# Chunks turned by VectorE's 32x32 transposes from rows loaded by quarters, and a landing wait at every fourth indirect transfer

## The chip, the cores and the metric

One core of a Trainium2 chip. The metric is the device time in microseconds, the median of several runs of the whole program. In the text PE is TensorE (the matrix engine), DVE is VectorE, ACT is ScalarE, POOL is GpSimd, and SP is SyncE, which here only issues transfers. "L374" is line 374 of the kernel.

## What is computed

The input `x` is 4 images of 32 channels, 128 x 128, float32. Layer 0 regroups each image into 128 channels (32 x 2 x 2) of 4096 pixels (64 x 64) and attends over the pixels: a 4096 x 4096 matrix of cosines, its softmax, and a weighted sum. Layer 1 takes the result as 4096 tokens of 128 per image: it is a linear attention without softmax, then a mixture of 8 experts with 2 chosen per token.

```python
def _L0_conv_ref(x, gamma):
    ...
    xs = x.reshape(B, C, h, R, w, R).transpose(0, 1, 3, 5, 2, 4).reshape(B, C * R * R, h, w)
    q = xs.reshape(B, C * R * R, hw)
    energy = jnp.einsum('bci,bcj->bij', q, q)
    d = jnp.sqrt(jnp.diagonal(energy, axis1=1, axis2=2))
    energy = energy / (d[:, :, None] * d[:, None, :])
    attn = jax.nn.softmax(energy, axis=-1)
    out = jnp.einsum('bcj,bij->bci', q, attn).reshape(B, C * R * R, h, w)
    out = gamma * out + xs
...
def _L1_attn_ref(x, Wk, Wq, Wv):
    ...
    KtV = jnp.einsum('bhnk,bhne->bhke', K, V)
    out = jnp.einsum('bhnk,bhke->bne', Q, KtV)
...
def _L1_ffn_ref(x, router_w, router_b, expert_w, expert_b):
    router_probs = jax.nn.softmax(x @ router_w + router_b, axis=-1)
    top_p, top_i = jax.lax.top_k(router_probs, K)
    top_p = top_p / jnp.sum(top_p, axis=-1, keepdims=True)
    expert_out = jnp.einsum('bnd,edc->bnec', x, expert_w) + expert_b
    ...
# layer 0, then for tokens t of its result:
    t = t + _L1_attn_ref(_ln_t(t), ...)
    t = t + _L1_ffn_ref(_ln_t(t), ...)
```

## The kernel before

**Layer 0.** For each of the 4 images the 4096 pixels are cut into 8 chunks of 512 (`NCH = 8`, `CH = 512`), and a chunk into 4 blocks of 128 (`NJ = 4`). Two forms of each chunk are kept: `qn`, channels by pixels with each pixel's vector scaled to length 1, and `qT`, pixels by channels, unscaled. `attend` (L416) walks over pairs of chunks (i, jc) with jc up to i: L557 makes the energies `pe` of one block against a chunk, L560 their exponentials `pr` on ACT with row sums, and L439 multiplies them with `qT` into `po` two steps later. The matrix is symmetric, so the other triangle is not computed. Instead L368 transposes `pr` in 32x32 blocks on DVE, L482 writes the result to a buffer in DRAM, and L494 reads it back with the 32-row groups exchanged, in six transfers on SP's queue. L374 (L395 for a diagonal tile) multiplies the returned tile, and L384 (L404) adds the product to the accumulator `o`. That use is scheduled `LAG = 57` units of a running count of matmul work after the read-back is issued.

**Preparing the chunks.** `prep(b, kc, st)` (L281) makes two chunks at a time, so it runs four times per image. It loads rows of the image in four transfers (`load_tokens`, L278), transposes them on PE in two groups of four 128x128 (L312), evicts each group on DVE into `qT` (L301), takes squares and row sums on DVE (L323, L324), raises the sums to the power -1/2 on POOL (`rn`, L163), scales `qT` into `qs` on DVE (L337), transposes `qs` back on PE in two groups of four (L345) and copies each to `qn` on ACT (L343). For the first chunk 22 filler transposes (`keep_running`) run on PE meanwhile.

**The order of work.** The order on PE, DVE, ACT and SP is the order in which the program emits it. The loop at L1348 steps through `attend`, whose every step yields twice, and at both it advances the streams that are due. A timed stream has a begin and an end, in per cent of the image's attention work, and a count: it comes due at even spacing, `count` times between the two, and is advanced twice each time. So a stream that yields n times is over after about n/2 counts. The preparation of the next image's chunks 0 and 1 runs late in an image, that of its chunks 2 and 3 early in the next.

**Layer 1** (L603) of an image runs as another stream beside the attention of the next image. It divides layer 0's accumulator (L710) and adds it to the tokens `T` (L732), normalises, attends, and chooses the experts. `sorted_experts` (L921) sorts the tokens of each half of an image by expert: 32 indirect transfers on POOL (L996) scatter rows of 128 tokens into `xs` in DRAM; SP loads the sorted tiles (L1022) once all have landed; PE transposes them (L1065) and multiplies them with the chosen expert (L1058); the products go to `ys`, and 32 more indirect transfers (L1123) gather them into `yb`; DVE combines (L1092). Each of these indirect transfers already waits for the exponential that was emitted last (`exps`), so that there are not more of them than attention steps. The last image's layer 1 takes another way, without sorting. `input_rows` (L594) loads the tokens `T` of an image.

Of the kernel before, what the change touches and what calls it, by code (L numbers as in the profile page):

```python
# [22 lines left out]
def kernel(  # L23
# [43 lines left out]
    nc = tc.nc  # L67
# [60 lines left out]
    def wait_for(inst, others, why):  # L128
        for other in others:
# [3 lines left out]
            )  # L133

# [146 lines left out]
    def prep(b, kc, st):  # L281

        if b == 0:
            if kc == 0:
                st["all"] = big1.tile([P, 4, 8, HW2, 2], F32, tag="T", name="xx_0")
            xx = st["all"][:, kc]
        else:
            xx = xin.tile([P, 8, HW2, 2], F32, tag="xx", name=f"xx_{b}_{kc}")
        first = b == 0 and kc == 0
        load_tokens(  # L290
            xx.rearrange("p k w r -> p k (w r)"), b, 8 * kc, 8, (nc.sync, nc.scalar if first else nc.sync)
        )
# [3 lines left out]
        yield  # L296
        yield
        yield from idle(2 if b else 1)

        def load_half(g, pt):  # L300
            nc.vector.tensor_copy(  # L301
                qT[:, :, 2 * g : 2 * g + 2, :].rearrange("p s j (r c) -> p (j r) s c", c=64),
                pt.rearrange("p (m s c) -> p m s c", s=2, c=64),
            )

        for g in range(2):
            yield
            pt, done = hold(f"ptq_{b}_{kc}_{g}", partial(load_half, g))
            for jj in range(2):
                for r2 in range(2):  # L310
                    k = 4 * g + 2 * jj
                    nc.tensor.transpose(  # L312
                        pt[:, ts(2 * jj + r2, P)], xx[:, k : k + 2, :, r2].rearrange("p k w -> p (k w)"), ident
                    )
            yield
            done()
        yield
# [3 lines left out]
        for s in range(2):  # L321
            sq = work.tile([P, NJ, P], F32, tag="qs", name=f"sq_{b}_{kc}_{s}", bufs=2)
            nc.vector.tensor_tensor(sq, qT[:, s], qT[:, s], ALU.mult)  # L323
            nc.vector.tensor_reduce(ss[:, ts(s, NJ)], sq, AX.X, ALU.add)  # L324
            if first:
                pow_neg_half(rn[:, ts(s, NJ), 0], ss[:, ts(s, NJ)])
            elif s == 1:
                pow_neg_half(rn[:, :, 0], ss)
            yield
            yield  # L330
        yield from idle(1)
        if first:
            keep_running(22, ps_g, "pg")
        scaled = []
# [1080 lines left out]
```

## Time and profile before

| | us |
|---|---|
| median of 3 runs | 1706.01 (1704.19 to 1707.77) |
| the profiled execution, its time | 1708.28 |
| the profiled execution, its span | 1706.5 |
| PE / DVE / ACT / POOL busy, 14 to 350 us (attention of image 0) | 333.8 / 141.9 / 168.5 / 9.0 |
| 350 to 757 us (image 1, layer 1 of image 0) | 399.0 / 232.9 / 226.7 / 142.5 |
| 757 to 1163 us (image 2) | 397.0 / 233.7 / 222.0 / 146.0 |
| 1163 to 1570 us (image 3) | 397.0 / 222.6 / 221.7 / 145.7 |
| 1570 to 1706 us (the last layer 1) | 118.3 / 98.8 / 84.4 / 65.1 |

The granted clock of TensorE is 0.994 over the span. The stretches of images are set by hand; an engine's busy time is the union of its instructions in the stretch. How the lines of the profile are read: a group line names the source line, engine, operation, what is written and read, the shapes and how many; then the busy time of the group, the mean of one in ns, and the idle time of the engine just before them with what ended it. A line of the timeline begins with start and duration.

### The profile page before, as it was taken

The numbers are of one execution on the slowest core, as the hardware profiler recorded it, in microseconds if no ns is written. First come the engines' busy times: TensorE is split into PE (matmuls) and PEld (weight loads), VectorE is DVE, ScalarE is ACT, GpSimd is POOL, SyncE is SP. The second block draws the span as 40 slices with busy tenths as digits, with TensorE's granted clock in tenths as the row PEclk, the third lists the DMA queues.
The fourth block names the chain that finished last, engine by engine and source line by source line (L and its number), as shares of the span: only waits on it lengthen the run. The fifth ranks groups of instructions, "written<-read, shape, count | busy, mean of one in ns | idle before, by whom it ended". The sixth has DMA issues, their size and how long they took to land.

```text
span 1706.5 us, 21941 instructions
## 1 busy us (share of the span) xinstructions
PE 1652.0 (97%) x5458; PEld 874.7 (51%) x5458; DVE 935.0 (55%) x2443; ACT 925.2 (54%) x2893; POOL 512.2 (30%) x553
## 2 busy tenths in 40 slices
PE   8999999999999999999999999999999999999898
PEld 5444544455554555445554455545555455544543
DVE  4433334467485345478477334557748533454686
ACT  3555445566565555446565455545657455544476
POOL 1000000011026425460015632443102642435157
PEclk9999999999999999999999999999999999999999
DMA  4554756754458778875457677886445877885001
GB/s 134 168 179 154 207 178 210 248 182 162 163 167 265 221 244 239 251 234 161 146 172 239 221 249 235 244 249 186 162 153 168 261 223 225 246 244 145 7 9 42
DMA packets 227341, 323.94 MB, mean 190 GB/s; under 512 B 31760, under 2 KB 155792, under 8 KB 213136
## 3 DMA queue, kind: packets, MB, share of 16 engines
q1 hardware_dynamic: 206704, 283.57, 52.5%
q0 software_dynamic: 12288, 25.19, 5.2%
q10 hardware_dynamic: 8224, 13.77, 2.8%
q8 instruction: 46, 0.75, 0.2%
q14 instruction: 79, 0.65, 0.1%
HBM read 152.28 MB, written 173.15 MB: 191 GB/s over the span
## 4 chain that ended last, share of the span: by engine, by line
PE 75%; DVE 9%; DMA 4%; issue 4%; ACT 4%; SPq 3%; POOL 1%; another core or an unknown queue 1%; ACTq 0%; DVEq 0%; POOLq 0%
PE pe L557 21%; PE po L439 21%; PE pg L374 17%; PE pys L1058 3%; PE py L1207 2%; PE pg L395 2%; SPq L494 2%; PE pys L1065 1%; DVE F L368 1%; PE pat L803 1%; DMA blocks<-F 1%; DMA F<-blocks 1%; ACT xn L645 1%; PE pgram L677 1%; DVE df L710 1%
## 5 line engine op out<-in xcount | busy, mean ns | idle before, releaser
L560 ACT ACTIVATE pr<-pe 128x512 f32<-128x512 f32 (+1 forms) x576 | 322.4, 560 | 548.9 <-PE pe L557 419.8
L439 PE MATMUL po<-pr,qT 128*128 128x512 f32 (+3 forms) x1152 | 552.2, 561 | 6.5 <-ACT o L444 6.0
L557 PE MATMUL pe<-qn,qn 128*128 128x512 f32 x896 | 462.3, 598 | 5.1 <-ACT pr L560 4.8
L374 PE MATMUL pg<-F,qT 128*128 128x512 f32 x864 | 441.9, 593 | 0.8 <-DMA F<-blocks 0.8
L368 DVE STREAM_TRANSPOSE F<-pr 128x512 f32<-128x512 f32 x440 | 306.1, 702 | 173.8 <-ACT pr L560 149.4
L439 PEld LDWEIGHTS po<-pr,qT 128*128 128x128 f32 x1152 | 216.1, 191 | 253.8 <-issue 223.0
L379 ACT ACTIVATE junk<-F 128x512 bf16<-128x512 f32 x432 | 267.9, 620 | 0.9 <-DMA F<-blocks 0.9
L374 PEld LDWEIGHTS pg<-F,qT 128*128 128x128 f32 x864 | 164.5, 191 | 193.8 <-issue 179.7
L1123 POOL DMA_INDIRECT yb<-ys,place x192 | 185.7, 967 | 252.8 <-ACT pr L560 72.6
L996 POOL DMA_INDIRECT xs<-xn,place x192 | 186.5, 971 | 162.3 <-ACT pr L560 83.7
L557 PEld LDWEIGHTS pe<-qn,qn 128*128 128x128 f32 x896 | 153.8, 191 | 114.5 <-issue 98.9
L384 DVE TENSOR_TENSOR o<-o,pg 128x512 f32<-128x512 f32 x110 | 75.4, 685 | 190.5 <-PE pg L374 153.3
L163 POOL TENSOR_TENSOR rn<-ss,neg_half 128x8 f32<-128x8 f32 (+1 forms) x17 | 26.9, 1586 | 332.2 <-DVE ss L324 332.1
L560 ACT ACTIVATION_READ_ACCUMULATOR pr<-pe 128x1 f32 x576 | 112.2, 195 | 0.0
L1032 ACT ACTIVATE xn<-pys 128x256 f32<-128x256 f32 x120 | 45.3, 378 | 112.6 <-PE pys L1065 80.7
L163 POOL TENSOR_TENSOR rsf<-dm_f,neg_half 128x8 f32<-128x8 f32 (+1 forms) x15 | 26.2, 1744 | 233.7 <-DVE sv_f L637 233.7
L1058 PEld LDWEIGHTS pys<-ew_sb,xn 128*128 128x128 f32 x468 | 69.4, 191 | 47.5 <-issue 43.1
L557 PE MATMUL pe<-qn 128*128 128x512 f32 (+3 forms) x256 | 90.5, 436 | 0.7 <-ACT qn L343 0.7
L379 ACT ACTIVATION_READ_ACCUMULATOR junk<-F 128x1 f32 x432 | 82.8, 192 | 0.0
L163 POOL TENSOR_TENSOR rsa<-dm_a,neg_half 128x8 f32<-128x8 f32 x16 | 26.4, 1649 | 185.3 <-DVE sv_a L637 184.9
L1041 DVE COPY xn<-pys 128x256 f32<-128x256 f32 x60 | 25.4, 424 | 91.1 <-ACT xn L1032 65.9
L1058 PE MATMUL pys<-ew_sb,xn 128*128 x468 | 71.8, 275 | 0.2
(216 smaller groups left out, 1623.5 us busy)
## 6 DMA issues: line engine op xcount, KB each, us to landing
blocks<-F SPq DMA_DIRECT2D x108, 1024.0 KB
F<-blocks SPq DMA_DIRECT2D x216, 192.0 KB
F<-blocks SPq DMA_DIRECT2D x216, 128.0 KB
xn<-xs SPq DMA_DIRECT2D x114, 128.0 KB
F<-blocks SPq DMA_DIRECT2D x216, 64.0 KB
below<-F SPq DMA_DIRECT2D x31, 384.0 KB
out_dram<-acc SPq DMA_DIRECT2D x128, 64.0 KB
xx<-in_x_dram SPq DMA_DIRECT2D x62, 128.0 KB
```

The costliest lines, as they stand in the source:

```text
L163: pinned(nc.gpsimd.tensor_tensor(dst, src, neg_half.to_broadcast(list(src.shape)), ALU.pow))
L368: f()
L374: nc.tensor.matmul(pg.rearrange("p (a f) -> p a f", a=4), st["qT"][i][:, ib, :], G[:, :, ib], start=(ib == 0), stop=(ib == NJ - 1),)
L379: nc.scalar.activation(junk, G[:, :, ib], AF.Copy, accum_out=st["sums"][:, NJ * i + ib, jc : jc + 1])
L384: nc.vector.tensor_tensor(o, o, pg.rearrange("p (a j c) -> p a j c", a=4, c=S), ALU.add)
L439: nc.tensor.matmul(row["po"][:, lo:hi], qT[blk // NJ][:, blk % NJ, :], w, start=start, stop=(row["left"] == 0))
L557: nc.tensor.matmul(pe[:, c0:], qn[jc][:, ts(j, P)], qn[i][:, c0:], start=True, stop=True)
L560: nc.scalar.activation(pr[:, c0:], pe[:, c0:], AF.Exp, accum_out=sums[:, t, i : i + 1]).ins
L996: inst = nc.gpsimd.indirect_dma_start(xs[h], offset(place[:, i, k : k + 1]), xn[:, k, :], None)
L1032: nc.scalar.activation(bufs[4 + g % 2][:, :n], p[:, : n * P].rearrange("p (j t) -> p j t", t=P), AF.Copy)
L1058: nc.tensor.matmul(p[:, 2 * P + j * D : 2 * P + j * D + D], bufs[4 + g % 2][:, j, :], weights[:, bass.ds(begins[2 * (g % 2) + j], D)], sta ...
L1123: inst = nc.gpsimd.indirect_dma_start(yb[k // 4][:, i, k % 4, :], None, ys, offset(place[:, i, k : k + 1]))
```

## The change

Chunks are made in another way, and the indirect transfers get another wait.

1. `load_quarters` loads the rows of two chunks in four transfers so that a quarter of the image rows stands on 32 partitions, 2 KB contiguous per row group, into one buffer `xa` (the pool's single buffer, shared with `xx`). `turn_quarters` makes `qT` of it with four 32x32-block DVE transposes of 128x256. The PE transposes at L312 and their evictions are gone. The pixels within a chunk now stand in another order, which `in_order` and `in_turn` and new access patterns in the division follow; the addition of L384 becomes contiguous, and the copies of `po` and the additions of `back` become permuted.
2. For all but the very first chunks, `qn` is no longer transposed from a scaled `qT`. The rows are loaded a second time, as before (`load_tokens` into `xx`; for image 0 straight into `T`), the factors `rn` are widened on DVE, transposed on PE in one group of four, and four DVE products of 64x512 read them from PSUM. The two ACT copies are gone.
3. The first chunks have their own `prep_first`, which still transposes `qn` on PE, with 40 filler transposes.
4. `T` of image 0 is loaded during the preparation; `input_rows` runs for images 1 to 3 only.
5. The preparation streams have new begins, ends and counts.
6. `landed_by_fours`: over both kinds of indirect transfer and all images, each fourth transfer waits until the one before it has landed.

```diff
+    moves = []
+
+    def landed_by_fours(inst):
+        if moves and len(moves) % 4 == 0:
+            wait_for(inst.ins, moves[-1:], "every fourth waits for all before it")
+        moves.append(inst.ins)
...
+    def load_quarters(b, kc, queues=(nc.sync, nc.sync)):
+
+        xa = xin.tile([P, 2, 2, 2, HW2, 2], F32, tag="xx", name=f"xa_{b}_{kc}")
+        halves = x[b].rearrange("c (s g) w -> c s (g w)", s=2)
+        for a in (0, 2, 1, 3):
+            first_row = 16 * kc + 4 * a
+            queues[a // 2].dma_start(
+                xa[ts(a, S)].rearrange("p s k r w e -> p s (k r w e)"),
+                halves[:, :, first_row * W : (first_row + 4) * W],
             )
-        for g in range(2):
-            yield
-            pt, done = hold(f"ptq_{b}_{kc}_{g}", partial(load_half, g))
-            for jj in range(2):
-                for r2 in range(2):
-                    k = 4 * g + 2 * jj
-                    nc.tensor.transpose(
-                        pt[:, ts(2 * jj + r2, P)], xx[:, k : k + 2, :, r2].rearrange("p k w -> p (k w)"), ident
-                    )
...
+    def turn_quarters(s, xa, qT):
+        for k in range(2):
+            nc.vector.transpose(
+                qT[:, s, 2 * k : 2 * k + 2, :].rearrange("p h (e r c) -> p r (h e) c", e=2, r=2),
+                xa[:, s, k].rearrange("p r (h t) e -> p (r h) e t", h=2),
+            )
+
+    def prep_first(st):
...
+        for s in range(2):
+            turn_quarters(s, xa, qT)
+            squares(b, kc, s, qT, ss)
+            pow_neg_half(rn[:, ts(s, NJ), 0], ss[:, ts(s, NJ)])
+        keep_running(40, ps_g, "pg")
...
+    def prep(b, kc, st):
+        ahead = 2 if b == 0 and kc == 1 else 5
+        xa = load_quarters(b, kc)
+        if b == 0:
+            load_tokens(st["T"][:, ts(kc, 8), :], b, 8 * kc, 8)
+            xx = rows_of_image(b, kc, st)
+        for _ in range(ahead):
+            yield
+        qT = chunks_of(b, kc, st)
+        for s in range(2):
+            turn_quarters(s, xa, qT)
+            yield
+        if b > 0:
+            xx = xin.tile([P, 8, HW2, 2], F32, tag="xx", name=f"xx_{b}_{kc}")
+            load_tokens(xx.rearrange("p k w r -> p k (w r)"), b, 8 * kc, 8)
...
+            for r2 in range(2):
+                nc.vector.tensor_tensor(
+                    qn[ts(r2, 64)].rearrange("p (j a t) -> p a j t", a=4, t=S),
+                    xx[own].rearrange("p (a k) (h t) r -> p r a (k h) t", a=4, h=2)[:, r2],
+                    view(spread[own]),
+                    ALU.mult,
+                )
...
+        for s in range(2):
+            squares(b, kc, s, qT, ss)
+            if s == 1:
+                pow_neg_half(rn[:, :, 0], ss)
+            yield
+        for _ in range(ahead - 2):
+            yield
+        wide = work.tile([P, NJ, 2, 64], F32, tag="qs", name=f"wide_{b}_{kc}", bufs=2)
+        for s in range(2):
+            nc.vector.tensor_copy(wide[:, :, s], rn[:, ts(s, NJ)].to_broadcast([P, NJ, 64]))
         yield
...
+        bank, done = hold(f"pnorm_{b}_{kc}", scale_all)
+        for j in range(NJ):
+            nc.tensor.transpose(bank[:, ts(j, P)], wide[:, j].rearrange("p s c -> p (s c)"), ident)
+        yield
+        done()
         yield
...
-                o = st["o"][jc].rearrange("p (j a c) -> p a j c", a=4, c=S)
-                nc.vector.tensor_tensor(o, o, pg.rearrange("p (a j c) -> p a j c", a=4, c=S), ALU.add)
+                nc.vector.tensor_tensor(st["o"][jc], st["o"][jc], pg, ALU.add)
...
-                    nc.scalar.activation(o, row["po"], AF.Copy)
+                    nc.scalar.activation(in_order(o), in_turn(row["po"]), AF.Copy)
...
                 wait_for(inst.ins, exps, "not more of these at a time than steps have")
+                landed_by_fours(inst)
                 scatters.append(inst.ins)
...
                 wait_for(pinned(inst).ins, exps, "not more of these at a time than steps have")
+                landed_by_fours(inst)
...
-            for kc, begin, end in ((1, 0, 5), (2, 6, 20), (3, 25, 45)):
-                timed.append((prep(0, kc, states[0]), begin, end, 12))
+            for kc, begin, end in ((2, 6, 22), (3, 25, 48)):
+                timed.append((prep(0, kc, states[0]), begin, end, 16))
...
-            timed.append((prep(b + 1, 0, nxt), 65, 82, 13))
-            timed.append((prep(b + 1, 1, nxt), 87, 99, 13))
-        begin, end, count = (52, 94, 17) if b == 0 else (36, 47, 9)
-        timed.append((input_rows(b, states[b]), begin, end, count))
+            timed.append((prep(b + 1, 0, nxt), 52, 78, 16))
+            timed.append((prep(b + 1, 1, nxt), 80, 99, 16))
+        if b > 0:
+            timed.append((input_rows(b, states[b]), 36, 47, 9))
...
-            timed.append((prep(b + 1, 2, nxt), 2, 20, 13))
-            timed.append((prep(b + 1, 3, nxt), 30, 50, 13))
+            timed.append((prep(b + 1, 2, nxt), 1, 22, 16))
+            timed.append((prep(b + 1, 3, nxt), 28, 52, 16))
```

## The prediction

> **What bounds the kernel.** I read the page's busy times and chain first, then the order of time on TensorE (PE) around its longest gaps, then the costs by form, then GpSimd's (POOL) indirect transfers.
>
> ```profile
> PE 1652.0 (97%) x5458; PEld 874.7 (51%) x5458; DVE 935.0 (55%) x2443; ACT 925.2 (54%) x2893; POOL 512.2 (30%) x553
> ...
> PE 75%; DVE 9%; DMA 4%; issue 4%; ACT 4%; SPq 3%; POOL 1%; another core or an unknown queue 1%; ACTq 0%; DVEq 0%; POOLq 0%
> ```
>
> PE is the bound: 97% busy, three quarters of the chain that ended last. Only PE time that goes, or a PE wait that comes or goes, moves the end. Busy time is not PE's price, though, because matmuls overlap; the distance between starts is. In order of time (start, duration, instruction, count, idle time before it):
>
> ```profile
> 721.34 1.02 PE L374 MATMUL pg<-F,qT 128*128 128x512 f32 x2
> ...
> 724.57 0.72 PE L312 MATMUL ptq<-ident,xx 128*128 128x128 f32 x4 [2.22 <-DMA xx<-in_x_dram]
> 725.13 1.02 PE L557 MATMUL pe<-qn,qn 128*128 128x512 f32 x2
> ...
> 727.71 0.63 PE L312 MATMUL ptq<-ident,xx 128*128 128x128 f32 x4
> 728.17 1.02 PE L557 MATMUL pe<-qn,qn 128*128 128x512 f32 x2
> ...
> 743.21 1.02 PE L374 MATMUL pg<-F,qT 128*128 128x512 f32 x2
> 747.30 0.66 PE L345 MATMUL ptn<-ident,qs 128*128 128x128 f32 x4 [3.07 <-issue]
> 747.79 1.46 PE L557 MATMUL pe<-qn,qn 128*128 128x512 f32 x2
> 749.04 1.91 PE L439 MATMUL po<-pr,qT 128*128 128x512 f32 x2
> 750.75 1.48 PE L374 MATMUL pg<-F,qT 128*128 128x512 f32 x2
> ```
>
> Two things are seen here. A group of four transposes moves the next matmul by 0.46 us (727.71 to 728.17), not by its 0.63; over all groups the median is 0.467 for L312 and 0.437 for L345. A pair of 128x512 records takes 0.86. And two of the worst PE gaps stand ahead of just these transposes: one waits for the input load, the other for VectorE (DVE). After the second, PE runs slowly for a while (749.04 to 750.75 is 1.71 in place of 0.86).
>
> **TensorE work that goes.** Each of the 15 later chunks loses four groups (two L312, two L345: 2 x 0.467 + 2 x 0.437 = 1.81 us) and gains one (0.437, as L345): 1.37 x 15 = **-20.6 us**. As busy time, the same 12 transposes of some 0.16 us would be 28 us; I take the pitch. The Trainium skill, VectorE: DVE Perf Modes, The three transpose paths, gives TensorE 390 ns for a 128x128 bf16 transpose; by that the 180 that go would be 70 us. No row here shows such a price in a stream, and it enters nothing.
>
> **TensorE waits that go.** Four stalls belong to the old chunk: at 721.34 (3.79 us to the second next start, where 0.86 + 0.467 are needed: 2.5 lost), 743.21 (7.54 to 750.75, 3.02 needed: 4.5), and their like one batch on, 1125.80 to 1133.58 (4.7) and 1150.12 to 1156.68 (4.4): 16.1 us. The first kind can't return in that form, since no PE instruction reads the input any more. The second is DVE's backlog from the division of layer 1 (L710, 2.78 us, then T L732, 1.22) falling on the last chunk's scaling. The new code moves that chunk: batch 1 runs from about 350 to 757 us (its four pow instructions of `rn`, at 407.6, 527.3, 657.5 and 738.7, stand at 14, 43, 76 and 95% of it), and the stream is advanced twice a count, so 15 yields end after 8 of 16 counts: at 90% (716 us) instead of 99%, ahead of the division at 739. Bounds: 0 (the new group waits for DVE's widening just as long) to -16.1. I take **-12**, nearer to the full amount, because the clash in time is gone, and leave 4 for new ones.
>
> **Start.** First matmul of attention now at 13.68 us. New: data at about 5.5, as now (again four loads of 128 KB, two on each queue), transposes 0.42 x 2 for the first half, squares 0.65 + 0.69, again for the second half, then one scaling (0.69): 5.5 + 4.4 + 0.7 = 10.6; four transposes 0.5, copy 0.6: 11.8. So -1.9 there. The 40 filler transposes end near 2 + 40 x 0.194 = 9.8 (the identity is ready at 1.8, and 22 took 4.27 now), just in time. But the second chunk's load shares its one buffer with the first, so SyncE's queue holds it to about 8.5 and it lands near 12; its norms then come at about 19.8, when PE asks at about 19.4. I take **-1.5**, bounds -2.5 and +3.
>
> **VectorE and ScalarE.** Costs by form (count, busy us, mean ns, idle before):
>
> ```profile
> L368 DVE STREAM_TRANSPOSE F<-pr 128x512 f32<-128x512 f32 x440 | 306.1, 702 | 173.8 <-ACT pr L560 149.4 <-issue 12.5 <-DMA F<-below 7.5
> ...
> L514 DVE STREAM_TRANSPOSE F<-pr 128x128 f32<-128x128 f32 x186 | 44.2, 283 | 22.8 <-ACT pr L560 20.1 <-issue 2.1 <-DMA F<-blocks 0.2
> L710 DVE TENSOR_TENSOR df<-o,pbd 64x512 f32<-64x512 f32 x64 | 44.0, 687 | 7.5 <-PE pbd L723 3.7 <-PE pe L557 2.6
> ...
> L337 DVE TENSOR_TENSOR qs<-qT,rn 128x512 f32<-128x512 f32 x32 | 20.6, 682 | 1.5 <-POOL rn L163 1.5
> ...
> L701 DVE TENSOR_SCALAR rdx<-rd,gam 128x256 f32<-128x256 f32 x32 | 10.5, 370 | 0.6
> ```
>
> Gone per chunk: two evictions (L301, 0.68) and two scalings (0.68), 2.72 us. Added: four 128x256 transposes (between L514's 0.28 and L368's 0.70; linear in columns gives 0.42, as taken: 1.68), two widenings (as L701, 0.37: 0.74), four 64x512 products out of PSUM (as L710, 0.687: 2.75). That is 5.17, so +2.45 x 15 = 37 us of DVE, from 935 to 972 (57%). At the transposes' upper bound it is 54. It costs nothing on the path: DVE idles 43% and works behind PE by the slack of six `pr` buffers. If that cover went, up to 37 us would show. ScalarE (ACT) loses two copies of 0.60 per chunk, 18 us, also hidden. The contiguous `o` additions (110 x 0.685) and the permuted copies (0.590) I leave at their old price: between 0 and -3 us for DVE, by the contiguous L323 row (0.656), off the path.
>
> **Loads.** Four more 128 KB loads per chunk of batches 1 to 3 (6 MB, SyncE issue of 0.45 us each), against 32 input loads of batch 0 that go (2 MB): under 2% of 324 MB. A load can hold SyncE's queue for the DVE transposes ahead of it (up to 3 us) and behind it wait L482 and L494, the round trip of the exponentials. Taken as 0: see the slack next.
>
> **The landing waits.** POOL and SyncE now:
>
> ```profile
> 550.21 0.96 POOL L996 DMA_INDIRECT xs<-xn,place  x1 [0.30 <-issue]
> ...
> 566.55 0.96 POOL L996 DMA_INDIRECT xs<-xn,place  x1 [5.26 <-ACT pr L560]
> ...
> 553.24 1.72 SPq L1022 DMA_DIRECT2D xn<-xs  x2
> 557.67 2.91 SPq L494 DMA_DIRECT2D F<-blocks  x6
> ```
>
> From the trace's packets (32 per transfer, in order) an indirect transfer lands 1.86 to 5.9 us after its start, mean 3.2. Back to back, starts are 1.27 apart. So four take 3 x 1.27 + 3.2 + 0.25 (the semaphore wait, an assumption from the 0.30 gaps) = 7.3 us, where the pace set by the exponentials is 6.2 (30 transfers from 502.13 to 548.95). Carrying every recorded start forward under the new rule, the last one of a half slips 9 to 12 us in the three first-half scatters, under 1 in the second-half ones, 3 to 8 in the six gathers: 68 us in all. What is queued behind: on POOL the pow instructions; on SyncE the load L1022 at 553.24, which waits for the scatter's landing and would move to about 563, and behind it L494 at 557.67. Cover: those blocks are first read by PE at 577.4 (shares are taken in order), 19.7 us after issue, while six transfers take some 6; the sorted rows are transposed at 569.2, 15.6 after their load ends; DVE's combine (L1092) comes 5 to 13 us after the landing of its row in most cases, 2.5 at the least. So nearly all is hidden: I take **+3**, bounds 0 and +68.
>
> The Trainium skill, DMA: Bandwidth & Descriptors, Anatomy of one DMA, gives a software-issued transfer 2.0 us + bytes/436e3, 2.15 us here. By it four would take 6.2, no lag at all; the trace's 3.2 differs and decides, and the page's figure enters no term.
>
> **Sum.** -20.6 - 12 - 1.5 + 3 = -31.1 us on the profiled execution (span 1706.5, time 1708.28): 1677.2. Its time is 2.27 above the median of the runs (1706.01), so the forecast for the median is **1675**.
>
> **Rivals.** (A) *The landing waits reach PE.* If a loaded queue lands the waited transfer about 1 us later than now, the gather halves (seven waits each) eat their 5 to 8 us of slack, DVE stands still in L1092, the transposes behind it come late, and PE follows. For: POOL already starts back to back for long stretches. Against: the slack above. With nothing hidden, 1675 - 3 + 68 = **1740**; it turns slower than before from about 34 us uncovered. 0.22. (B) *VectorE takes over* where slices show it at 8 tenths: its 37 us are paid, 1675 + 37 = **1712**, and 1706 if part of it. Against: the L384 and L368 rows wait for others 190 and 174 us. 0.07. (C) *The stalls only move*: PE waits as long for the widening as it did for L337; 1675 + 12 = **1687**. 0.15. That the new code doesn't do what it says I exclude: each removed transpose stands in the diff.
>
> **How the numbers follow.** Forecast 0.56, with its own range 1665 to 1684: at the low end all 16.1 us of stalls go (-4), the landing waits cost nothing (-3), the start gives -2.5; at the high end some 9 us of new waits. The range begins at 1662, for the 3 us of the contiguous additions, and goes up to 1708, which leaves out most of A. 0.2% is 3.4 us, about what can be told from no change. Faster: forecast, C and a little of B, 0.72; same 0.05, out of A and B; slower 0.23.
>
> **What would show it.** Right: 3 groups fewer per chunk, PE busy near 1625, no stall over 2 us at the scaling transposes, L1022 ten microseconds later after the first-half scatters, no new PE gap at L374. Wrong: idle PE before L374 or the sorted transposes with a DMA as releaser, DVE idle before L1092 with the gather as releaser, or long gaps before the new norm transposes.

## The result, and the profile after

The changed kernel takes 1752.1 us (median, 1746.22 to 1755.87) beside 1705.62 us of the kernel before: a ratio of 1.0269, 95% interval 1.0249 to 1.0289. It is slower by 46 us, and outside the range of 1662 to 1708. The profiled execution took 1751.13 us, with a span of 1749.4 and a granted clock of 0.979 (0.994 before).

From the costs by group of the kernel before:

```profile
L1092 DVE SCALAR_TENSOR_TENSOR acc<-yb,weight,acc 128x128 f32<-128x128 f32 x192 | 65.8, 344 | 3.6
...
L645 ACT ACTIVATE xn<-T,nba,rsa 128x128 f32<-128x128 f32 x120 | 49.2, 483 | 17.2 <-POOL nba L639 13.4 <-issue 3.8
...
L677 PE MATMUL pgram<-xn 128*128 128x128 f32 x256 | 35.0, 280 | 3.8 <-ACT xn L645 2.6 <-issue 1.1
```

From the page and the costs by group of the kernel after:

```profile
PE 1637.8 (94%) x5288; PEld 861.0 (49%) x5288; DVE 965.1 (55%) x2535; ACT 910.9 (52%) x2863; POOL 513.4 (29%) x553
...
L1155 DVE SCALAR_TENSOR_TENSOR acc<-yb,weight,acc 128x128 f32<-128x128 f32 x192 | 65.6, 342 | 86.8 <-DMA yb<-ys,place 73.5 <-issue 7.2 <-DMA G<-F 2.7
L707 ACT ACTIVATE xn<-T,nba,rsa 128x128 f32<-128x128 f32 x120 | 49.1, 483 | 66.5 <-POOL nba L701 66.5
L739 PE MATMUL pgram<-xn 128*128 128x128 f32 x256 | 39.7, 304 | 51.3 <-ACT xn L707 51.0
...
L322 DVE STREAM_TRANSPOSE qT<-xa 128x256 f32<-128x256 f32 x64 | 23.5, 412 | 11.3 <-DMA xa<-in_x_dram 5.7 <-PE po L501 5.6
L378 DVE TENSOR_TENSOR qn<-xx,pnorm 64x512 f32<-64x512 f32 x48 | 32.7, 682 | 1.7 <-PE pnorm L403 0.9 <-issue 0.2
L394 DVE COPY wide<-rn 128x256 f32<-128x256 f32 x30 | 7.0, 275 | 1.1 <-POOL rn L170 1.1
```

PE has 170 matmul records and 14 us fewer than before, as planned, and yet its share fell from 97% to 94%: the span is 43 us longer, and PE's idle time grew from 54.5 to 111.6 us. Three groups tell on whom. DVE's combine (L1155, before L1092) idled 3.6 us before and 86.8 now, 73.5 of them for gathered rows. ACT's normalisation (L707, before L645) waited 13.4 us for POOL before and waits 66.5 now. The Gram sums on PE (L739, before L677) waited 2.6 us for ACT before and wait 51.0 now.

The timeline of the same kernel around the longest of PE's waits (start, duration, instruction, idle time before it):

```profile
741.93 1.02 PE L437 MATMUL pg<-F,qT 128*128 128x512 f32 x2
...
749.14 0.17 DVE L698 TENSOR_SCALAR dm_a<-dm_a 128x8 f32<-128x8 f32 x1
...
751.28 0.95 POOL L1186 DMA_INDIRECT yb<-ys,place  x1 [4.46 <-DVE acc L1155]
...
754.32 0.96 POOL L1186 DMA_INDIRECT yb<-ys,place  x1 [2.08 <-issue]
755.59 0.95 POOL L1186 DMA_INDIRECT yb<-ys,place  x1 [0.30 <-issue]
756.85 0.95 POOL L1186 DMA_INDIRECT yb<-ys,place  x1 [0.30 <-issue]
757.00 0.35 DVE L1155 SCALAR_TENSOR_TENSOR acc<-yb,weight,acc 128x128 f32<-128x128 f32 x1 [2.71 <-DMA yb<-ys,place]
...
760.33 0.95 POOL L1186 DMA_INDIRECT yb<-ys,place  x1 [2.53 <-issue]
761.58 0.95 POOL L1186 DMA_INDIRECT yb<-ys,place  x1 [0.30 <-issue]
762.55 1.68 POOL L170 TENSOR_TENSOR rsa<-dm_a,neg_half 128x8 f32<-128x8 f32 x1
764.30 0.20 POOL L701 TENSOR_TENSOR nba<-sv_a,rsa 128x8 f32<-128x8 f32 x1
764.54 0.49 ACT L707 ACTIVATE xn<-T,nba,rsa 128x128 f32<-128x128 f32 x1 [21.97 <-POOL nba L701]
764.94 1.25 ACT L707 ACTIVATE xn<-T,nba,rsa 128x128 f32<-128x128 f32 x3
...
765.08 2.08 PE L739 MATMUL pgram<-xn 128*128 128x128 f32 x8 [19.56 <-ACT xn L707]
```

Read it backwards. PE waits 19.56 us for ACT, ACT waits 21.97 us for POOL's `nba`, and `nba` follows the power at 762.55, which takes 1.68 us. That power waits for no operand: `dm_a` was written at 749.31, 13.2 us earlier. It stands in POOL's queue behind gathers that wait for landings (at 751.28 the profile names the combine that frees the buffer, but that gather too starts 1.13 us after the landing before it). In the kernel before, each of the 16 powers of these statistics starts 0.08 or 0.09 us after its operand; here the first one of three images starts 13.2, 11.2 and 10.6 us after it. The same stall returns at 1184.56 us (15.90) and 1603.18 us (12.86).

The diff puts the wait at scatters and gathers, but within a half only the gathers have it. POOL's timeline after, first in a scatter, then in a gather:

```profile
502.86 1.03 POOL L1058 DMA_INDIRECT xs<-xn,place  x1 [0.20 <-issue]
504.19 0.96 POOL L1058 DMA_INDIRECT xs<-xn,place  x1 [0.30 <-issue]
505.46 0.96 POOL L1058 DMA_INDIRECT xs<-xn,place  x1 [0.30 <-issue]
506.72 0.97 POOL L1058 DMA_INDIRECT xs<-xn,place  x1 [0.30 <-issue]
508.00 0.96 POOL L1058 DMA_INDIRECT xs<-xn,place  x1 [0.31 <-issue]
509.26 0.96 POOL L1058 DMA_INDIRECT xs<-xn,place  x1 [0.30 <-issue]
...
656.74 0.94 POOL L1186 DMA_INDIRECT yb<-ys,place  x1 [5.05 <-DMA yb<-ys,place]
657.99 0.94 POOL L1186 DMA_INDIRECT yb<-ys,place  x1 [0.30 <-issue]
659.24 0.95 POOL L1186 DMA_INDIRECT yb<-ys,place  x1 [0.30 <-issue]
660.50 0.95 POOL L1186 DMA_INDIRECT yb<-ys,place  x1 [0.31 <-issue]
666.37 0.95 POOL L1186 DMA_INDIRECT yb<-ys,place  x1 [4.93 <-ACT pr L623]
```

Six scatters in a row start some 1.26 us apart, so none waits for a landing. Of the 47 scatters at every fourth place 36 start before the one ahead of them has landed, by the trace's packets; of the 42 such gathers inside the halves none does. Each scatter is put into a group of instructions that are declared free of order among themselves (`add_to_no_dep_group`, L1063), and in the program the new dependency between two members of one group is not there. The halves of the scatters last about as long as before (47.1 and 60.4 us in the first image, 48.1 and 59.0 before). The gathers stop at every fourth, and their halves last 66.4, 67.6, 69.2, 65.8, 70.0 and 57.9 us, before 52.3, 54.3, 53.5, 57.3, 53.3 and 48.6.

The 0.95 us of a gather's row is not its transfer: by the trace's packets the waited gathers land 3.4 to 4.0 us after their start on average in five of the six halves, 2.3 in the last. The Trainium skill, Perfetto Trace Analysis, DMA Instruction — SWDGE (GPSIMD), says that the row of such an instruction ends when its descriptors are written, not when the data has moved; these rows agree. The next gather doesn't start at the landing either: it starts 1.04 to 1.63 us after the last packet of the one that it waits for, 1.23 on average over the 42 waits.

### The profile page after: what moved, and what is told of

Read it like the earlier page. It is cut to its first block, busy times and chain, and to the rows that moved or that the text cites. A ratio compares the mean times of both kernels' runs of the same rounds, so it can differ in the third digit from the quotient of the medians.

```text
span 1749.4 us, 21642 instructions
## 1 busy us (share of the span) xinstructions
PE 1637.8 (94%) x5288; PEld 861.0 (49%) x5288; DVE 965.1 (55%) x2535; ACT 910.9 (52%) x2863; POOL 513.4 (29%) x553
## 2 busy tenths in 40 slices
DMA packets 227853, 330.22 MB, mean 189 GB/s; under 512 B 32272, under 2 KB 152208, under 8 KB 213648
## 5 line engine op out<-in xcount | busy, mean ns | idle before, releaser
L1155 DVE SCALAR_TENSOR_TENSOR acc<-yb,weight,acc 128x128 f32<-128x128 f32 x192 | 65.6, 342 | 86.8 <-DMA yb<-ys,place 73.5
L620 PE MATMUL pe<-qn 128*128 128x512 f32 (+3 forms) x256 | 94.2, 451 | 0.7 <-ACT qn L348 0.7
L739 PE MATMUL pgram<-xn 128*128 128x128 f32 x256 | 39.7, 304 | 51.3 <-ACT xn L707 51.0
L707 ACT ACTIVATE xn<-T,nba,rsa 128x128 f32<-128x128 f32 x120 | 49.1, 483 | 66.5 <-POOL nba L701 66.5
```

What stands on the lines that cost most here:

```text
L620: nc.tensor.matmul(pe[:, c0:], qn[jc][:, ts(j, P)], qn[i][:, c0:], start=True, stop=True)
L739: nc.tensor.matmul(p[:, :D], xn[:, k, :], xn[:, k, :], start=(k == rows[0]), stop=(k == rows[-1]))
L1155: nc.vector.scalar_tensor_tensor(a[:, k % 4, :], yb[k // 4][:, i, k % 4, :], weight[:, i, k, :], a[:, k % 4, :], ALU.mult, ALU.add)
```

## The experiments

The runs were made on several chips; each stands beside runs of the kernel before on its own chip, and ratios are to those. Before took 1697 to 1702 us on them. Where two versions are subtracted, it is said on which chip.

### Wait and chunks apart

`a_no_landing_wait`: the changed kernel without the wait, at both kinds of transfer.

```diff
-                landed_by_fours(inst)
```

> The changed kernel without the landing waits; all else kept. Theory L (the waits, which act in the gathers only, let GpSimd fall behind; the power of layer 1's statistics queues behind the late gathers and the normalisation and TensorE stand still, three times 13 to 20 us, plus VectorE's 74 us of waits in the combine): the three stalls before the Gram matmuls go, VectorE's idle time before the combine falls under 10 us, time 1680 to 1695. Rival D (the new chunks themselves are dear: VectorE's added work, the norm transposes' waits, the start): it stays above 1725, and the stalls move but do not go.

1713.76 us, ratio 1.0071 (1.0045 to 1.0097). The three stalls before the Gram sums are gone and DVE no longer idles in the combine. But the new chunks without the wait are no gain; they were to give 34 us, and the time lies between the two ranges expected.

`b_before_with_wait`: the kernel before with the wait and nothing else.

```diff
+                landed_by_fours(inst)
```

> The kernel before, with the landing waits alone added. Theory L: 40 to 60 us slower than before, 1746 to 1766, with TensorE stalls at layer 1's Gram matmuls in three images. Rival D: within 15 us of before, 1706 to 1720. Rival I (neither part alone, only both together, since the new schedule puts other work on the same stretch): within 10 us of before here, and a_no_landing_wait also near 1706 or under.

1735.55 us, ratio 1.0178 (1.0143 to 1.0212): 33 us for the wait alone, on the same chip, less than theory L's 40 to 60 and more than its rival's 15. PE's timeline there, at the end of image 1:

```profile
751.38 1.12 PE L352 MATMUL ptn<-ident,qs 128*128 128x128 f32 x4 [6.18 <-DVE qs L344]
...
767.51 2.08 PE L684 MATMUL pgram<-xn 128*128 128x128 f32 x8 [8.17 <-ACT xn L652]
```

Here the lag reaches PE twice, through DVE (whose combine idles 60.6 us for gathered rows, and whose other work queues behind it) and through POOL and ACT.

`f_sliding`: as many gathers in flight at most, but no drain; each waits for the fourth before it.

```diff
-        if moves and len(moves) % 4 == 0:
-            wait_for(inst.ins, moves[-1:], "every fourth waits for all before it")
+        if len(moves) >= 4:
+            wait_for(inst.ins, moves[-4:-3], "each waits for the fourth before it")
```

> The changed kernel, but each gather waits for the landing of the fourth before it, in place of every fourth waiting for the one just before. At most four are in flight in both. Theory L with the drain as its cause (the landing of 3.3 us stands between two starts once in four): four starts take 5.1 us back to back, more than a landing, so nearly no wait shows and the time is within 5 us of a_no_landing_wait. Rival F (the limit of four in flight is what costs, drained or not): within 10 us of the changed kernel, 1740 to 1755.

1713.14 us, ratio 1.0055 (1.003 to 1.0079), no more than without any wait. Four in flight are enough; the standstill until the last of them has landed is what costs.

`h_later_normalise`: the wait kept, the step that consumes POOL's powers eight empty steps later for the first quarter of the rows.

```diff
-            yield from idle(1 if late_rows else 2)
+            yield from idle(1 if late_rows else 10 if kc == 0 else 2)
```

> The changed kernel with its landing waits; layer 1's normalisation of the first quarter of an image is emitted eight advances (some 20 us) later after its statistics, for images 0 to 2 (10 in place of 2). Theory L: the power, late by some 13 to 20 us on GpSimd's queue, is then in time; the three long stalls at the Gram matmuls go, and the time falls by 35 to 50 us, to 1700 to 1717. Rival V (VectorE's waits in the combine are the loss, and the stalls only where it shows): the stalls stay or come out elsewhere, and the time stays above 1735.

In this kernel the Gram sum of the first quarter is copied over what later quarters had added, so part of the sum is left out of the result. 1743.25 us, ratio 1.0244 (1.0209 to 1.0279). The theory that the late powers alone are the cost falls: the stall before the Gram sums is gone, and in PE's timeline another stands close by.

```profile
773.63 1.11 PE L785 MATMUL pbd<-ident,rdx 128*128 128x128 f32 x4 [15.91 <-DVE rdx L763]
```

DVE's divisors are late there, because DVE stands in the combine (100.2 us of idle time for gathered rows). POOL's lag comes out wherever the next engine that works in order meets it.

### The wait against the pace

`g_by_eights`: the wait at every eighth transfer.

```diff
-        if moves and len(moves) % 4 == 0:
+        if moves and len(moves) % 8 == 0:
```

> The changed kernel with the wait at every eighth transfer by index instead of every fourth. Theory P (pace): what counts is whether a group with its drain lasts longer than the program takes to emit it; four gathers then cost 3 x 1.27 + 3.5 + 0.25 = 7.6 us against an emission of about 6.6 us per four, and the lag grows; eight cost 7 x 1.27 + 3.5 + 0.25 = 12.6 us against about 13.3, so that nearly no lag builds up: 1711 to 1722 us, and the first PE stall before the Gram sums (19.7 us at 745 us) under 4 us. Rival L (each drain costs its share): half as many drains cost half of the 38 us, 1728 to 1738 us, and the stall near 10 us.

1699.31 us, ratio 1.0012 (0.9999 to 1.0025), on a second chip. The version without the wait takes 0.992 of before on a chip of the same kind (below; neither of the two shows the idle rows told of at the end), so eights cost some 16 us, where half of the 42 that fours cost would be 21. The stall near 742 us lost 5.9 us, between the 4 of theory P and the 10 of its rival. It leans to P, but "nearly no lag" was too much. (The microseconds expected here and for the next run start from the first chip, where the version without the wait is slower, so the ratio to 0.992 is what counts.)

`m_slower_gathers`: waits at every fourth, and two empty steps after every fourth gather.

```diff
+                if n % 4 == 3:
+                    yield
+                    yield
```

> The changed kernel, waits kept at every fourth gather, but the gathers are emitted more slowly: two empty steps after every fourth. Theory P: with the emission slower than a group with its drain no lag builds up on POOL, the powers and the combines are not late, and the time comes near the version without the wait: 1711 to 1724 us, although exactly as many drains are paid. Rival L (each drain is paid in the time): 1740 us or more. A second way to fail: the combines come later by the empty steps and the next stage waits for them, which would show as PE waiting for the last combine.

1685.76 us, ratio 0.9924 (0.9898 to 0.995): with exactly the same drains, some 0.03 of before under the changed kernel. DVE's idle time in the combine fell from 86.8 to 13.3 us. What is left is one stall of 12.4 us at 1580.83, before layer 1 of the last image: DVE still stands in the combine, because the last of the slower gathers of image 2 start as late as 1577.60.

`r_before_slower`: the kernel before, with the slower pace for images 0 and 1.

```diff
+                if n % 4 == 3 and b < 2:
+                    yield
+                    yield
```

> The kernel before, with nothing of the change, but two empty steps after every fourth gather of images 0 and 1. If gathers in a row hold up POOL's powers and the combines in the kernel before too, 3 to 10 us go (0.994 to 0.998). Rival: its old preparation sets the end of those images, and nothing changes (0.998 to 1.002).

1689.79 us, ratio 0.9946 (0.9928 to 0.9963): the slower pace is worth some 9 us in the kernel before too. So `m_slower_gathers` doesn't show that the drains cost nothing: a gain of the pace itself may be in its time. The reason given isn't shown: ACT waits for POOL's powers no less than before (14.6 us against 13.4).

### The chunks: density or place

`k_old_windows`: no wait, the preparation's windows of before. (Its expectation speaks of the count of before; that was 13. Eight counts, as run, spread the 16 steps over the whole window.)

```diff
-            timed.append((prep(b + 1, 0, nxt), 52, 78, 16))
-            timed.append((prep(b + 1, 1, nxt), 80, 99, 16))
+            timed.append((prep(b + 1, 0, nxt), 65, 82, 8))
+            timed.append((prep(b + 1, 1, nxt), 87, 99, 8))
...
-            timed.append((prep(b + 1, 2, nxt), 1, 22, 16))
-            timed.append((prep(b + 1, 3, nxt), 28, 52, 16))
+            timed.append((prep(b + 1, 2, nxt), 2, 20, 8))
+            timed.append((prep(b + 1, 3, nxt), 30, 50, 8))
```

> No landing wait, the new chunks, but the preparation's four windows and its count as in the kernel before (65 to 82, 87 to 99, 2 to 20, 30 to 50, eight steps each). Theory W: part of the missing gain lies in where the new windows put the work (the fourth against the routing chain: +4 us in images 1 and 2): 5 to 15 us under the version without the wait, 1699 to 1709 us. Rival: the new chunks themselves (more VectorE instructions in a row in front of evictions) cost it wherever they stand: 1709 to 1725 us.

1671.92 us, ratio 0.9848 (0.9822 to 0.9874): 25 us faster than before. Its page:

```profile
PE 1625.4 (97%) x5288; PEld 856.1 (51%) x5288; DVE 964.4 (58%) x2535; ACT 913.5 (55%) x2863; POOL 509.8 (31%) x553
```

The same 5288 matmuls keep PE busy for 12 us less than in the changed kernel: fewer run after a stall at a lowered clock (granted clock 0.994 here, 0.979 there).

`n_spread`: no wait, the new windows, eight counts in place of sixteen.

```diff
-            timed.append((prep(b + 1, 0, nxt), 52, 78, 16))
+            timed.append((prep(b + 1, 0, nxt), 52, 78, 8))
```

(and so for the other three)

> No landing wait, the new chunks in the new windows (52 to 78, 80 to 99, 1 to 22, 28 to 52), but eight counts in place of sixteen, so that a chunk pair's 16 steps fill the whole window instead of its first half. Theory D (density): what costs is that the steps follow each other so closely that PE's norms are asked for while VectorE still works at the widening; spread out, the stalls go, and the time comes near that with the old windows (0.985 of before): 0.980 to 0.992 of before. Rival L (place): the new windows lie against the routing chain and the division wherever their steps fall: 1.000 to 1.008 of before, as with sixteen counts (1.007).

1672.5 us, ratio 0.9847 (0.9825 to 0.9869), the same as with the old windows (on another chip, where before is within 0.2%): it is the density, not the place. In the changed kernel a stream of 15 steps that is advanced twice a count is through after half of its window.

`i_norms_later`: no wait, the dense steps kept, the transposes of the widened norms two steps later.

```diff
             nc.vector.tensor_copy(wide[:, :, s], rn[:, ts(s, NJ)].to_broadcast([P, NJ, 64]))
         yield
+        yield
+        yield
```

> No landing wait, and in each of the 15 chunk pairs the PE transposes of the widened norms (pnorm) are emitted two steps later than in the changed kernel. Theory S: of the 45 us by which the new chunks fall short (11 us slower than before instead of 34 faster) a good part is PE standing at pnorm for VectorE's widening copy: 1.9 us before the norms at 509 us, and again near 918 and 1330 us, 2.4 us at 22.7 us, each followed by some 2 us in which the pairs of matmuls last 1.7 us at a slow pitch. With two steps more the wait goes at those places: 8 to 16 us under the version without the wait, 1698 to 1706 us. Rival: the backlog is VectorE's as a whole at those places (norm group, routing chain and evictions in one row), and the wait moves to the next PE instruction that needs VectorE: within 5 us of the version without the wait (1709 to 1719).

1680.94 us, ratio 0.9895 (0.9866 to 0.9924), on the second chip. Beside the 1.0071 of the first chip it looks like 30 us, beside the 0.992 of a like chip it is some 4, which can't be told from none. The waits for the norms did go: 0.3 us in all, where `a_again`, the same version without the two steps, has 7.4. So this run doesn't settle what share the norms have. That they wait is plain in PE's timeline, here of `a_third`, the version without the wait:

```profile
507.13 1.02 PE L437 MATMUL pg<-F,qT 128*128 128x512 f32 x2
510.02 0.66 PE L403 MATMUL pnorm<-ident,wide 128*128 128x128 f32 x4 [1.86 <-DVE wide L394]
...
511.08 1.63 PE L620 MATMUL pe<-qn 128*128 128x384 f32 x2
512.50 1.81 PE L501 MATMUL po<-pr,qT 128*128 128x512 f32 x2
514.15 1.02 PE L437 MATMUL pg<-F,qT 128*128 128x512 f32 x2
```

PE stands 1.86 us for the widening, and of the next two pairs the first takes 1.42 and the second 1.65 us to the next start, where 0.72 and 0.86 are usual. In `n_again`, on the same chip, the norms come elsewhere and PE doesn't stop between 503 and 515 us.

`l_wait_old_windows`: the changed kernel with its wait, and the four timed streams as in `k_old_windows`.

```diff
+            timed.append((prep(b + 1, 0, nxt), 65, 82, 8))
...
                 landed_by_fours(inst)
```

> The changed kernel with its landing waits, in the windows that gave 0.985 without them (65 to 82, 87 to 99, 2 to 20, 30 to 50, eight counts). If the waits cost the same wherever the chunks stand, as they did in the kernel before (+33 us) and in the changed one (+38 us): 30 to 40 us more, 1.003 to 1.009 of before. Rival: the waits' cost was mostly a meeting of the gathers' lag with the dense new chunks: 15 us or less, 0.985 to 0.994.

1727.88 us, ratio 1.0177 (1.0151 to 1.0204), 55 us above `n_spread` on the same chip: more than expected, and the rival (a meeting of the lag with the dense chunks) falls. That more of the lag shows where PE goes faster (33, 42 and 55 us in three versions) is argued only, since the three stand on different chips.

### All parts on one chip

`a_again`: the program of `a_no_landing_wait`, on the chip of `n_spread`.

> The changed kernel without the landing wait once more, beside the others. If the stalls of PE at 551 and 960 us, where ScalarE stood for several us without a releaser, belong to the program, they are there again and the time is 1.005 to 1.010 of before; if they belong to the first chip, they are gone and the time is 0.999 to 1.003.

1683.93 us, ratio 0.992 (0.989 to 0.995) in place of 1.0071. Prices taken across chips are therefore not sound, and the three that matter were run on one chip: the changed kernel (`after_again`), without the wait (`a_third`), and without the wait and with spread steps (`n_again`). Their edits are those above.

> The changed kernel as it is, once more, so that it, the version without the wait and the version with spread steps stand on one chip. If the 1.5% between the two measurements of the version without the wait belongs to the chip alone, and this chip is like the second: 1.010 to 1.020 of before. If it is like the first: 1.025 to 1.029.

> The changed kernel without the landing wait, on the same chip. The wait's price is the difference to the changed kernel: 33 to 56 us in the other versions, 30 to 45 us here. The rest against the spread steps is the price of the dense steps: 12 us where the stalls without a releaser are absent (0.992 of before), up to 38 us where they are there (1.007).

> The spread steps in the new windows, without the wait, on the same chip: 0.983 to 0.987 of before on either kind of chip if spread steps leave PE the slack to bear the stalls without a releaser, as the kernel before does; above 0.995 on a chip that shows them if they don't.

| on one chip | us | ratio to before (95%) |
|---|---|---|
| before | 1700.44 | |
| after_again: wait, dense steps | 1752.34 | 1.0308 (1.0287 to 1.0329) |
| a_third: no wait, dense steps | 1710.78 | 1.0047 (1.003 to 1.0063) |
| n_again: no wait, spread steps | 1686.44 | 0.992 (0.9904 to 0.9937) |

So the wait costs 41.6 us, the dense steps 24.3, and the rest of the change gives 14.0: together +51.9. On the chip of `a_again` and `n_spread` the dense steps cost 12 us (0.992 against 0.9847) and the rest gives 26. Where the 24 us lie shows in part in what PE waited for (us in total, times, longest), first in `a_third`, then in `n_again`:

```profile
PE pe L620 <- ACT pr L623: 19.4, 15, 3.3
PE pnorm L403 <- DVE wide L394: 7.7, 4, 2.1
...
PE pnorm L403 <- DVE wide L394: 5.6, 2, 3.1
PE pe L620 <- ACT pr L623: 4.0, 7, 0.7
```

With 2.3 us that the profile gives no releaser for, the norms cost 7.9 us in `n_again`, no less than with dense steps. PE's waits for exponentials make the difference here. On the chip of `a_again` and `n_spread` it is the other way: 3.1 and 1.6 us for exponentials, 7.4 and 2.5 for the norms. How the dense steps make the exponentials late on one chip stays open. My expectation that spread steps would be as fast here as there fell: 0.992 is neither in the first range nor above the bound of the second.

### Versions that beat both

`o_norms_later_old_windows`: no wait, old windows with nine counts, norms two steps later, 58 fillers.

```diff
-        keep_running(40, ps_g, "pg")
+        keep_running(58, ps_g, "pg")
...
+        yield
+        yield
...
+            timed.append((prep(b + 1, 0, nxt), 65, 82, 9))
```

> No landing wait, the old windows with nine counts, the transposes of the norms two steps later, and 58 filler transposes at the start instead of 40. Without the wait the old windows gave 0.985 of before; left there are about 2.5 us before the output products near 20 us, 4 us near 718, 2.7 at 1112 and 4.7 us at the start. If the norms' lateness is behind them too: 3 to 8 us less, 0.980 to 0.983. Rival: the two steps push the scaling past the end of its window into the next chunk's, and nothing is gained: 0.984 or more.

1668.85 us, ratio 0.9825 (0.9809 to 0.9841), not told apart from 0.9847 (0.9825 to 0.9869).

`o2_and_slower_gathers`: the same with the slower pace of `r_before_slower`.

> The version with later norms and old windows, and two empty steps after every fourth gather of images 0 and 1. With the waits the slower gathers alone took 66 us off (1.027 to 0.992 of before). Theory: part of that is that gathers issued back to back delay POOL's powers and the combines even without any wait; then 3 to 8 us under its twin. Rival: without the wait there is no lag left to remove, and the empty steps change nothing (within 3 us) or make the moved rows late at the end of the image (slower by 2 us or more).

1661.93 us, ratio 0.9782 (0.9765 to 0.9799): 7 us under its twin, and the fastest version, 2.2% under before.

`q_slower_with_wait`: the same with the landing wait put back.

```diff
+                landed_by_fours(inst)
```

> The version with old windows, later norms and slower gathers in images 0 and 1 (0.978 of before), with the landing wait at every fourth gather put back. Theory P (pace): the wait costs nothing where the program takes longer to emit four gathers than the four take to land; only image 2, whose gathers are still emitted at the old pace, may pay, some 13 to 17 us at the most as in the last image of the other versions with the wait: 0.978 to 0.988 of before. Rival: the slower pace only gave room of its own, and the wait still costs the 33 to 56 us that it cost in three other versions: 0.998 or more.

1682.92 us, ratio 0.9918 (0.9889 to 0.9947): by the ratios 23 us above the same version without the wait, on the same chip; P allowed 17, and its range was passed, but the rival's 33 to 56 is not reached. Where it is paid shows in PE's timeline of this one execution:

```profile
735.02 1.64 PE L741 MATMUL pgram<-xn 128*128 128x128 f32 x8 [2.28 <-ACT xn L709]
...
1532.69 2.08 PE L741 MATMUL pgram<-xn 128*128 128x128 f32 x8 [13.41 <-ACT xn L709]
```

The gathers of images 0 and 1 are slowed: the stall is 2.28 us at the first, and at the second, 1126.52 us, there is none. Those of image 2 come at the old pace with the same wait, and the stall is 13.41. The gathers' own times say the same: the halves of images 0 and 1 last 71.3 to 73.3 us with the wait and 71.1 to 73.1 without it (`o2_and_slower_gathers`), those of image 2 69.0 and 60.1 with it and 51.5 and 46.1 without. The wait is nearly free where the program takes longer to emit four gathers than they take to land. The profiled execution took 1677.07 us, 15.7 more than its twin's, and PE's idle time in it is 15.0 us longer (48.5 and 33.5), so in that execution the price is placed, most of it at image 2. The other executions took 1681 to 1689 us; what they have more isn't placed.

## Why the prediction was wrong

**The landing waits: +3 predicted, 41.6 measured. This is the step that failed.** Of rival A the mechanism was right in part (DVE stands still in the combine) and its price was an upper bound; it had 0.22. Its condition, landings about 1 us later, didn't come: every fourth gather landed 3.35 us after its start before and lands 3.53 after it now, averaged over the halves. And PE's long stalls come through POOL's powers, which it doesn't name. Three things were wrong in the term.

- Its pieces: four gathers were to take 7.3 us against a pace of 6.2, which is that of the scatters. In the first half of image 0's gathers the gap at a wait is 5.17 us on average, so four take 3 x 1.26 + 5.17 = 8.9 us, and the pace of the gathers before was 52.3/31 x 4 = 6.7. The landing was taken at 3.2 and is 3.99 in this half; the larger error is the time from the landing to the next start, assumed to be 0.25 us and 1.23 on average. Seven waits a half at 1 us more each, added to the slips of 3 to 8 that were worked out, make 10 to 15 us (an estimate); the halves last 8 to 17 us longer.
- Its cover: the slack was read for the combine, the sorted rows and the blocks. The powers on POOL were named as queued behind and then given no slack at all. They had none: ACT waited 13.4 us for them before already. The Gram sums behind them waited 2.6 us before and wait 51.0 now.
- Its place: the slips of 9 to 12 us in the scatters don't exist. "That the new code doesn't do what it says I exclude" was argued from the transposes alone; the wait at the scatters isn't in the program. The load L1022, expected to move from 553.24 to about 563, stands at 553.54 (L1085).

**TensorE work: -20.6 predicted, borne out as far as it can be seen.** Matmul records fell by 170, and a norm group moves the next start by 0.44 us (0.437 predicted). PE busy is 1625.4 us in `k_old_windows`, without the long stalls, where 1625 was named. In image 0, where layer 1 and the wait are absent, the changed kernel is 6.2 us ahead at the last copy of `o`; five of the chunk pairs at 1.37 and 1.5 for the start make 8.4, of which about 2 come back in the next point.

**Stalls that go: -12 predicted.** The four old stalls went, but the reason ("the clash in time is gone") looked only at what the moved step leaves. That the stream is through after 8 of 16 counts was seen and used to place it; what it means that its steps thereby stand close to each other was not asked. They gave back 24 us on one chip and 12 on another. Rival C, priced at 12, names PE's wait for the widening; on the second of these chips spreading the steps takes 5 us of that wait away, on the first none, so it is at most a part. With the steps spread, the chunks give 14 and 26 us of the predicted 34.

**Loads: 0.** The 2 MB of batch 0 that were set against the new loads don't go, they are loaded in the preparation, and the bytes grew by 6.3 MB (323.94 to 330.22). It enters no term.

**Start: -1.5.** The first matmul of attention came at 11.93 us (11.8 predicted). By PE's timeline the fillers end at 7.97, not near 9.8, PE then stands 2.62 us, and the first pair lasts 2.07 us; then the second chunks' norms wait 2.38 us at 22.67. By the second copy of `o` nothing is left.

**VectorE and ScalarE: right, and hidden.** DVE is at 965 us (972 predicted), with the transposes at 0.412 us (0.42), the widening at 0.275 (0.37) and the products at 0.682 (0.687). ACT lost 14 of the 18 us. Rival B has no row for it: with spread steps DVE is as busy, and the kernel is faster than before.

## What to carry to other kernels

In these runs a wait for a landing cost little where the program emitted a group more slowly than the group and its wait took. Where it didn't, the excess added up over the whole run of groups, and it was paid by whatever stood behind in that queue, however small. Count into a wait the time from the landing to the next start, and measure it. So list everything that the waiting engine issues next, and read the slack of each consumer, the least first. When work is spread by a count, check how many steps one count makes: the same windows at half the count were worth 12 to 24 us.

## What the runs showed of the hardware that wasn't expected

- **One program, different chips.** The version without the wait took 1.0071, 1.0047 and 0.992 of the kernel before on three chips, while before itself differed by 0.2% between them. The program was measured once on each, so that the chip itself makes the difference isn't shown. The two slower chips show idle time that the profile puts down to no engine or queue of this core, at the same place of the program. ACT's timeline, `a_third`:

```profile
549.74 0.31 ACT L461 ACTIVATE junk<-F 128x128 bf16<-128x128 f32 x1
549.95 0.19 ACT L461 ACTIVATION_READ_ACCUMULATOR junk<-F 128x1 f32 x1
555.00 0.60 ACT L623 ACTIVATE pr<-pe 128x512 f32<-128x512 f32 x1 [4.86 <-remote]
```

  On the first chip the same row stands at 554.07 with 4.86 us. On the faster chip ACT waits 0.85 us there, for PE, and no such row is found in the whole trace. The kernel before has such rows too in its profile, six of them with 24.6 us in all, while PE waits only 4.8 us for exponentials in it. What ACT waits for, and why only on some chips, stays open.

- **PE slows after short gaps, not always.** After 1.86 us of idle time at 510.02 the pairs took 1.42 and 1.65 us, and the granted clock is 0.50 from 510.66 to 514.08; in `a_again`, after the same 1.86 us at 507.73, the same two forms took the usual 0.72 and 0.86, and the granted clock is 1.00 throughout from 500 to 515. The Trainium skill, TensorE: Matmul & The Clock Gate, Part 1: The HAM clock gate (the "warmup" mystery), has the clock drop after an idle window of about 3.4 us that runs freely. Stretches of the lowered clock in these traces do last 3.41 us or a multiple (6.83 us at 555.03 in `a_third`, 20.48 at 749.11 in the changed kernel); but here a gap of about half that length is followed by one. What decides between the two runs isn't shown.
